# The last stage of a factorization kernel: x² times the summed W² as one level of Strassen's algorithm

## Chip, cores and metric

The kernel runs on one core of one Trainium2 chip. The metric is device time in microseconds (us) of one execution; the number for a kernel is the median of its runs.

## What is computed

x has 1024 rows and 512 features, the weight is 64 matrices W[e] of 512 x 512, all in float32. Cut to what matters:

```python
out_lin = x @ lin_w.T + lin_b
xv = jnp.einsum('bf,efm->bem', x, weight)
zp = jnp.einsum('bf,efm->bem', jnp.square(x), jnp.square(weight))
interaction = 0.5 * jnp.sum(jnp.square(xv) - zp, axis=1)
return out_lin + interaction
```

The sum over e of zp is one product: square(x) times the sum over e of square(W[e]). So the kernel computes 64 products x W[e], squares and adds them, and one more product, x² (sum of W²), at the end. The output is 1024 x 512: half the sum of squares, minus half of that last product, plus the linear layer.

## The kernel before

**Stages.** At the start come the linear layer (`lin`, L172) and the sums of blocks of x. Then a loop over 32 pairs of matrices (`q`, L404): a pair is one 512 x 1024 matrix, and x times it is done by two nested levels of Strassen's algorithm in the Winograd form, with 7 products instead of 8 at each level. The outer level has seven block products in the order "1265734" (L393), each of which consists of seven inner products named "1" to "7" (`block_product`, L288).

An inner product (`product`, L274) is two matmuls of 128 x 128 by 128 x 256 into the halves of one PSUM bank. A block product uses three banks, x, v and y, as running sums: "1" and "2" go to x, "5" and "3" to v, and y begins as a copy of x after "1" and then gains "6", "7" and "4". Between two products a bank is read out by ScalarE or VectorE (`out_of`, `join`), since the intermediate sums are blocks of the result. So a later product into a bank must wait until the earlier state has been read. PSUM has 2 buffers for tag x and 3 each for v and y.

GpSimd makes the sums of weight blocks (`outer_t` L226 for the outer level, `inner_t` L246 for the inner one), and it also issues the accumulating DMAs: the four finished blocks of a pair, z5, c11, c12 and c21, are squared in place by ScalarE (`squares`, L361) and then added to `acc[0]` (c11, c12) or `acc[1]` (z5, c21) by a DMA with an add. The squared weights (`w_squares`, L373) are added to `w2_sum` in the same manner. An accumulating DMA waits for the earlier one on the same destination.

**What sets the order.** Nothing is reordered by a scheduler: each piece of work is put in a list with a due time (`st.at(t, fn)`), the list is sorted by that time, and each engine receives its instructions in that order and works them off in order. One unit of due time is one inner product: a pair takes 49 units for its 49 products. The products of one block stand two units apart, and those of its neighbours lie between them. The last pair begins at 49 * 31, the list ends soon after 49 * 32. For the last block product of the last pair ("4", `t0` = 49 * 32 - 7) the list places its inner products at t0 + 0, 2, 4, 6, 8, 10 and 12, and the accumulations of z5, c12 and c21 five units after their squares.

**The last stage** follows the list (L453 to L478). x has been loaded again and squared (`load_xq`, `square_xq`, two instructions of 128 x 2048). For each of 8 blocks of 128 rows, four matmuls of 128 x 128 by 128 x 512 form the product (L462) in one of three banks of tag v. VectorE makes o = 0.5 acc + bias (L469) and then o - 0.5 ps (L477), and one DMA stores 128 rows of 2 KB (L478):

```python
nc.vector.scalar_tensor_tensor(o, ps, -0.5, o, ALU.mult, ALU.add)
nc.sync.dma_start(out_dst[:, n, :], o)
```

Tiles rotate through pools: `zpool` has 6 buffers, `spool` 3 of each tag, `w2pool` 2, `wpool` 4, `topool` 3.

Of the kernel before, what the change touches and what calls it, by code (L numbers as in the profile page):

```python
# [8 lines left out]
F32 = mybir.dt.float32  # L9
AF = mybir.ActivationFunctionType  # L10
ALU = mybir.AluOpType
# [17 lines left out]
def kernel(  # L29
# [30 lines left out]
    nc = tc.nc  # L60
    _, _, _, Q = x.shape
    E, F, M = weight.shape
    P = 128
    NK = F // P
    NB = 4 * Q // P
    HM = M // 2
    BK = 2 * HM

    const = ctx.enter_context(tc.tile_pool(name="const", bufs=1))
    wpool = ctx.enter_context(tc.tile_pool(name="wpool", bufs=4))  # L70
    topool = ctx.enter_context(tc.tile_pool(name="topool", bufs=3))
    tipool = ctx.enter_context(tc.tile_pool(name="tipool", bufs=3))
    w2pool = ctx.enter_context(tc.tile_pool(name="w2pool", bufs=2))
    spool = ctx.enter_context(tc.tile_pool(name="spool", bufs=3))
    zpool = ctx.enter_context(tc.tile_pool(name="zpool", bufs=6))
    psum = ctx.enter_context(
        tc.tile_pool(name="psum", bufs=3, space=bass.MemoryType.PSUM)
    )
# [4 lines left out]
    w2_sum = const.tile([P, NK, M], F32, tag="w2_sum", name="w2_sum")  # L83
    acc = [
        const.tile([P, 4, BK], F32, tag=f"acc{r}", name=f"acc{r}") for r in range(2)
    ]
# [4 lines left out]
    st = Stream()  # L91
# [7 lines left out]
    BLOCK = {"1": (0, 0), "2": (0, 1), "4": (1, 1)}  # L99
    a21 = {i: raw_sb[:, n, :] for n, i in enumerate("124")}  # L100
# [89 lines left out]
    def rows(n):  # L190

        r, s, j = n // 4, n // 2 % 2, n % 2
        return acc[r][:, 2 * s : 2 * s + 2, ts(j, HM)]
# [92 lines left out]
    Z = {}  # L286
# [74 lines left out]
    def squares(t, q, name, r):  # L361
        def sq():
            z = Z[q, name]
            for h in range(2):
                o = z[:, ts(h, 2)]
                nc.scalar.activation(o, o, AF.Square)  # L366

        st.at(t, sq)
        st.at(
            t + 5, lambda: nc.gpsimd.dma_start(acc[r], Z[q, name], accum_op=ALU.add)  # L370
        )

    def w_squares(t, q, v):  # L373
# [29 lines left out]
    NQ = E // 2  # L403
    for q in range(NQ):  # L404
        g0 = 49 * q
        st.at(-100 if q == 0 else g0 - 48.8, lambda q=q: load_w(q))
        for n, i in enumerate(ORDER):
            t0 = g0 + 7 * n
            lead = t0 - 7.5
            if i == "6":  # L410
                st.at(lead - 8, lambda q=q: outer_t(q, "5"))
                st.at(lead - 4, lambda q=q: outer_t(q, "6"))
            if i == "7":
                st.at(lead - 4, lambda q=q: outer_t(q, "7"))
            if i == "4":
                st.at(lead - 1, lambda q=q: outer_t(q, "4"))
            st.at(lead, lambda q=q, i=i: inner_t(q, i))
            block_product(t0, q, i, SUMS[i])
            if i == "2":
                squares(t0 + 14.6, q, "c11", 0)  # L420
            if i == "7":
                squares(t0 + 14.6, q, "z5", 1)
            if i == "3":
                squares(t0 + 14.6, q, "c12", 0)
            if i == "4":
                squares(t0 + 14.6, q, "c21", 1)
        for v in range(2):
            w_squares(g0 + 14.6 + 14 * v, q, v)
# [4 lines left out]
            st.at(t + 0.1 * n, fn)  # L433


    xq = []

    def load_xq():
        for r in range(2):
            xq.append(wpool.tile([P, 2, 4, Q], F32, tag="w", name=f"xq{r}"))  # L440
            nc.sync.dma_start(xq[r], x[:, ts(r, 2)])

    def square_xq(r):
        nc.scalar.activation(xq[r], xq[r], AF.Square)

    st.at(49 * NQ - 48.8, load_xq)
    for r in range(2):
        st.at(49 * NQ - 20 + 5 * r, lambda r=r: square_xq(r))

    with tc.manual_schedule():  # L450
        st.run()

    bias_sb = w2pool.tile([P, M], F32, tag="w2", name="bias_sb")  # L453
    nc.sync.dma_start(bias_sb, lin_b.partition_broadcast(P))
    out_dst = out.rearrange("(n p) m -> p n m", p=P)
    for n in range(NB):
        r, s, j = n // 4, n // 2 % 2, n % 2
        ps = psum.tile([P, M], F32, tag="v", name=f"ps_out{n}", bufs=3)
        o = spool.tile([P, M], F32, tag="s5", name=f"o{n}")
        for k in range(NK):  # L460
            kk, l = k // 2, k % 2
            nc.tensor.matmul(  # L462
                ps,
                xq[r][:, kk, (0, 1, 3, 2)[2 * s + l], ts(j, P)],
                w2_sum[:, k, :],
                start=(k == 0),
                stop=(k == NK - 1),
            )
        nc.vector.scalar_tensor_tensor(  # L469
            o.rearrange("p (u c) -> p u c", u=2),  # L470
            rows(n),
            0.5,
            bias_sb.rearrange("p (u c) -> p u c", u=2),
            ALU.mult,
            ALU.add,
        )
        nc.vector.scalar_tensor_tensor(o, ps, -0.5, o, ALU.mult, ALU.add)  # L477
        nc.sync.dma_start(out_dst[:, n, :], o)  # L478


# [28 lines left out]
```

## Time and profile before

| | |
|---|---|
| median of 3 runs | 1421.89 us (1421.57 to 1421.89) |
| the profiled execution | 1422.3 us, span 1420.5 us, granted TensorE clock 1.0 |
| last stage on TensorE (L462) | 1389.25 to 1416.73 us from the span's start, 64 records |
| last matmul of the pairs (L277) | starts within the group at 1388.15 us |
| GpSimd in the pairs' part, 50 to 1350 us | 1106.7 of 1300 us busy |
| GpSimd from 1395 us on | 0 busy |
| an accumulating DMA, issue to landing | 7.6 us (median of acc<-z_c) |

Times in views are us from the start of the span; a profile's row gives start, duration, engine, line, operation, the tiles (out<-in), the shape, how often, and in brackets how long the engine sat idle before and what ended that. PE is TensorE, DVE is VectorE, ACT is ScalarE, POOL is GpSimd, SP issues loads and stores. A float32 matmul leaves two MATMUL records. Matmuls overlap in the pipeline, so that the distance from start to start says more than the duration of one.

### The profile page before, as it was taken

The numbers are of one execution on the slowest core, as the hardware profiler recorded it, in microseconds if no ns is written. First come the engines' busy times: TensorE is split into PE (matmuls) and PEld (weight loads), VectorE is DVE, ScalarE is ACT, GpSimd is POOL, SyncE is SP. The second block draws the span as 40 slices with busy tenths as digits, with TensorE's granted clock in tenths as the row PEclk, the third lists the DMA queues.
The fourth block names the chain that finished last, engine by engine and source line by source line (L and its number), as shares of the span: only waits on it lengthen the run. The fifth ranks groups of instructions, "written<-read, shape, count | busy, mean of one in ns | idle before, by whom it ended". The sixth has DMA issues, their size and how long they took to land.

```text
span 1420.5 us, 17935 instructions
## 1 busy us (share of the span) xinstructions
PE 1415.3 (100%) x6408; PEld 1221.2 (86%) x6408; DVE 916.8 (65%) x1333; ACT 610.8 (43%) x811; POOL 1153.8 (81%) x1027
## 2 busy tenths in 40 slices
PE   9999999999999999999999999999999999999998
PEld 4888888888888888888888888888888888888884
DVE  7666666665666665666765666766666666566664
ACT  1444444444444445444345444344444444444451
POOL 4688888888888888988888888888888888888870
PEclk9999999999999999999999999999999999999999
DMA  4499898889998889888899988988988888988975
GB/s 177 107 194 215 198 202 200 187 191 216 200 201 202 184 197 214 198 200 198 194 193 203 207 200 197 201 186 194 215 200 200 200 187 189 217 200 200 202 161 148
DMA packets 39976, 276.15 MB, mean 194 GB/s; under 512 B 4432, under 2 KB 4816, under 8 KB 7248
## 3 DMA queue, kind: packets, MB, share of 16 engines
q0 software_dynamic: 27504, 200.29, 69.4%
q1 hardware_dynamic: 11808, 72.62, 17.2%
q10 hardware_dynamic: 576, 2.10, 0.4%
q8 instruction: 51, 0.84, 0.2%
q14 instruction: 37, 0.30, 0.1%
HBM read 72.61 MB, written 2.10 MB: 53 GB/s over the span
## 4 chain that ended last, share of the span: by engine, by line
PE 100%; DVE 0%; issue 0%
PE y L277 41%; PE x L277 27%; PE v L277 27%; PE ps_out L462 2%; PE lin L182 2%; PE y_spin L170 0%; DVE o L477 0%; DVE zero L167 0%
## 5 line engine op out<-in xcount | busy, mean ns | idle before, releaser
L277 PE MATMUL y<-ti,xs 128*128 128x256 f32 x2688 | 653.8, 379 | 0.0
L277 PEld LDWEIGHTS y<-ti,xs 128*128 128x128 f32 x2688 | 511.8, 190 | 68.8 <-issue 0.7
L342 ACT COPY y<-x 128x512 f32<-128x512 f32 x224 | 127.7, 570 | 622.8 <-PE x L277 622.8
L277 PE MATMUL x<-to,xs 128*128 128x256 f32 x1024 | 252.4, 379 | 0.0
L277 PE MATMUL v<-ti,xs 128*128 128x256 f32 x896 | 230.0, 379 | 0.0
L277 PEld LDWEIGHTS x<-to,xs 128*128 128x128 f32 x1024 | 195.0, 190 | 26.0
L251 POOL TENSOR_TENSOR ti<-to 128x512 f32<-128x512 f32 x128 | 180.7, 1412 | 44.2 <-PE y L277 40.7
L237 POOL TENSOR_TENSOR to<-w,to 128x1024 f32<-128x1024 f32 x64 | 158.9, 2483 | 45.7 <-PE v L277 45.7
L366 ACT ACTIVATE z_c<-z_c 128x1024 f32<-128x1024 f32 x192 | 192.7, 1053 | 3.1 <-DVE z_c L337 2.3
L277 PE MATMUL x<-w,xs 128*128 128x256 f32 x768 | 191.9, 379 | 0.0
L277 PEld LDWEIGHTS v<-ti,xs 128*128 128x128 f32 x896 | 170.6, 190 | 22.7
L337 DVE TENSOR_TENSOR z_z<-y,s 128x512 f32<-128x512 f32 x128 | 88.0, 687 | 130.4 <-PE y L277 130.4
L277 PEld LDWEIGHTS x<-w,xs 128*128 128x128 f32 x768 | 146.3, 190 | 19.9 <-issue 0.5
L251 POOL TENSOR_TENSOR ti<-w 128x512 f32<-128x512 f32 x96 | 130.9, 1364 | 30.6 <-PE y L277 20.2
L370 POOL DMA_DIRECT2D acc<-z_c x96 | 83.6, 871 | 63.7 <-ACT z_c L366 52.1
L277 PE MATMUL v<-to,xs 128*128 128x256 f32 x512 | 131.4, 379 | 0.0
L321 DVE TENSOR_TENSOR s<-y,z_z 128x512 f32<-128x512 f32 x160 | 110.3, 689 | 28.9 <-PE y L277 23.1
L382 ACT ACTIVATE w<-w 128x1024 f32<-128x1024 f32 x126 | 126.3, 1054 | 0.0
L337 DVE TENSOR_TENSOR z_c<-y,s 128x512 f32<-128x512 f32 x96 | 66.4, 692 | 87.9 <-PE y L277 87.9
L321 DVE TENSOR_TENSOR s<-v,z_z 128x512 f32<-128x512 f32 x160 | 110.1, 688 | 18.0 <-PE v L277 11.0
L337 DVE TENSOR_TENSOR z_z<-v,s 128x512 f32<-128x512 f32 x128 | 87.7, 685 | 38.6 <-PE v L277 38.6
L277 PEld LDWEIGHTS v<-to,xs 128*128 128x128 f32 x512 | 97.5, 190 | 13.0
(57 smaller groups left out, 1574.1 us busy)
## 6 DMA issues: line engine op xcount, KB each, us to landing
acc<-z_c POOLq DMA_DIRECT2D x96, 1024.0 KB, 7.6
w_sum<-w POOLq DMA_DIRECT2D x63, 1024.0 KB, 8.6
w<-weight SPq DMA_DIRECT2D x62, 1024.0 KB, 5.9
acc<-z_z POOLq DMA_DIRECT2D x32, 1024.0 KB, 7.7
xq<-x SPq DMA_DIRECT2D x2, 1024.0 KB, 5.6
out<-o SPq DMA_DIRECT2D x8, 256.0 KB, 2.0
xs<-x SPq DMA_DIRECT2D x3, 384.0 KB, 7.7
lw_sb<-lin_wT ACTq DMA_DIRECT2D x2, 512.0 KB, 6.6
```

Of the source, the lines that this page charges most:

```text
L182: nc.tensor.matmul(LIN[n], quarter(r, kk, (0, 1, 3, 2)[2 * s + l])[:, ts(j, P)], lw_sb[:, 2 * kk + l, :], start=(kk == 0 and l == 0), stop ...
L237: nc.gpsimd.tensor_sub(t, a, b)
L251: nc.gpsimd.tensor_sub(t[:, 0:2, :], b[:, :, HM:M], b.rearrange("p l m -> p (l m)")[:, 0:M].rearrange("p (u c) -> p u c", u=2),)
L277: nc.tensor.matmul(ps[:, ts(j, HM)], xsl(i, o)[:, ts(j, P)], rhs, start=(start and j == 0), stop=True, skip_group_check=True,)
L321: nc.vector.tensor_add(o, d[bank], Z[q, addend][:, blk])
L337: nc.vector.tensor_add(Z[q, name][:, blk], d[bank], d[s])
L342: st.at(t0 + 0.5, lambda: nc.scalar.copy(d["y"], d["x"]))
L366: nc.scalar.activation(o, o, AF.Square)
L370: t + 5, lambda: nc.gpsimd.dma_start(acc[r], Z[q, name], accum_op=ALU.add)
L382: nc.scalar.activation(w2[:, ts(h, 2)], W[q, v][:, ts(h, 2)], AF.Square)
L462: nc.tensor.matmul(ps, xq[r][:, kk, (0, 1, 3, 2)[2 * s + l], ts(j, P)], w2_sum[:, k, :], start=(k == 0), stop=(k == NK - 1),)
```

## The change

The last stage becomes one level of the same Winograd form, with x² cut into 2 x 2 blocks (rows r, features kk) and the sum of W² into 2 x 2 blocks (features kk, columns u). It is run twice, for the two halves s of the rows of a block. A product `last_product` is four matmuls of 128 x 128 by 128 x 256 (j over two groups of 128 rows, l over two of 128 features), so one half has 28 of them. Here P1 to P7 are its products, in the order 1, 5, 6, 2, 7, 3, 4; they use banks x, v, y as a block product does: P1 and P2 to x, P5 and P3 to v, y begins as ScalarE's copy of x after P1 and gains P6, P7 and P4.

- GpSimd computes the four sums of blocks of x² (`last_sx`, 128 x 1024 each) and the four of W² (`last_tw`, 128 x 512 each), at due times within the last pair. `last_sx` needs the squared x, `last_tw` the finished `w2_sum`.
- The list places the products of s=0 from g on (g = 49 * 32), the first ones between those of the last block "4", and those of s=1 from g + 10 on.
- For s=0, ScalarE reads the states v after P5, y after P6, x after P2 and y after P4 out, times -0.5 (`scaled`), and VectorE combines y after P7 and v after P3 with them (`minus_half`). Four `last_t` (0.5 acc + bias, for s=0) are added later by two `add_t` of 128 x 1024.
- For s=1, four `last_t` come first, and VectorE reads all six states out (`minus_half`), with t as addend where s=0 had none.
- In the VectorE list the four `last_t` of s=1 stand at g + 10.2, the six read-outs of s=1 at g + 12.5, 14.5, 16.5, 18.5, 20.5 and 22.5, and the `last_t` of s=0 and the `add_t` at g + 16.6 to 16.9.
- The bias has a buffer of its own and is loaded right after x. x² is squared in four instructions of 128 x 1024. For the last pair the accumulations stand two units after their squares, not five.
- A store is 128 x 2 rows of 1 KB; there are eight of them, as before.

```diff
--- before.py
+++ after.py
@@ -62,7 +62,6 @@
     E, F, M = weight.shape
     P = 128
     NK = F // P
-    NB = 4 * Q // P
     HM = M // 2
     BK = 2 * HM
 
@@ -367,7 +366,8 @@
 
         st.at(t, sq)
         st.at(
-            t + 5, lambda: nc.gpsimd.dma_start(acc[r], Z[q, name], accum_op=ALU.add)
+            t + (5 if q < NQ - 1 else 2),
+            lambda: nc.gpsimd.dma_start(acc[r], Z[q, name], accum_op=ALU.add),
         )
 
     def w_squares(t, q, v):
@@ -433,49 +433,166 @@
             st.at(t + 0.1 * n, fn)
 
 
-    xq = []
+    g = 49 * NQ
+    h = g - 49
+    XQ, SX, TW = [], {}, {}
+    bias = const.tile([P, M], F32, tag="bias", name="bias")
 
     def load_xq():
         for r in range(2):
-            xq.append(wpool.tile([P, 2, 4, Q], F32, tag="w", name=f"xq{r}"))
-            nc.sync.dma_start(xq[r], x[:, ts(r, 2)])
-
-    def square_xq(r):
-        nc.scalar.activation(xq[r], xq[r], AF.Square)
-
-    st.at(49 * NQ - 48.8, load_xq)
+            XQ.append(wpool.tile([P, 2, 4, Q], F32, tag="w", name=f"xq{r}"))
+            nc.sync.dma_start(XQ[r], x[:, ts(r, 2)])
+        nc.sync.dma_start(bias, lin_b.partition_broadcast(P))
+
+    def square_xq(r, kk):
+        nc.scalar.activation(XQ[r][:, kk], XQ[r][:, kk], AF.Square)
+
+    def last_x(i):
+        if i in BLOCK:
+            r, kk = BLOCK[i]
+            return XQ[r][:, kk]
+        return SX[i]
+
+    def last_sx(i):
+        if i in "57":
+            SX["tile" + i] = w2pool.tile([P, 2, 4, Q], F32, tag="w2", name=f"sx{i}")
+        SX[i] = SX["tile5" if i in "56" else "tile7"][:, "5673".index(i) % 2]
+        a21, a22 = XQ[1][:, 0], XQ[1][:, 1]
+        if i == "5":
+            nc.gpsimd.tensor_add(SX[i], a21, a22)
+        elif i == "6":
+            nc.gpsimd.tensor_sub(SX[i], SX["5"], last_x("1"))
+        elif i == "7":
+            nc.gpsimd.tensor_sub(SX[i], last_x("1"), a21)
+        else:
+            nc.gpsimd.tensor_sub(SX[i], last_x("2"), SX["6"])
+
+    def last_b(kk, u):
+        return w2_sum[:, ts(kk, 2), ts(u, HM)]
+
+    def last_tw(i):
+        if i in "57":
+            TW["tile" + i] = topool.tile([P, 2, 2, HM], F32, tag="to", name=f"tw{i}")
+        TW[i] = TW["tile5" if i in "56" else "tile7"][:, "5674".index(i) % 2]
+        a, b = {
+            "5": lambda: (last_b(0, 1), last_b(0, 0)),
+            "6": lambda: (last_b(1, 1), TW["5"]),
+            "7": lambda: (last_b(1, 1), last_b(0, 1)),
+            "4": lambda: (last_b(1, 0), TW["6"]),
+        }[i]()
+        nc.gpsimd.tensor_sub(TW[i], a, b)
+
+    def last_w(i):
+        if i in "123":
+            return last_b(*{"1": (0, 0), "2": (1, 0), "3": (1, 1)}[i])
+        return TW[i]
+
+    def last_product(ps, i, s, start):
+        for j in range(2):
+            for l in range(2):
+                nc.tensor.matmul(
+                    ps[:, ts(j, HM)],
+                    last_x(i)[:, (0, 1, 3, 2)[2 * s + l], ts(j, P)],
+                    last_w(i)[:, l, :],
+                    start=(start and j == 0 and l == 0),
+                    stop=True,
+                    skip_group_check=True,
+                )
+
+    out_dst = out.rearrange("(r s j p) (u c) -> r s p u j c", r=2, s=2, j=2, u=2)
+    L = {}
+
+    def last_banks(s):
+        for n in "xvy":
+            L[n, s] = psum.tile(
+                [P, BK], F32, tag=n, name=f"{n}_last{s}", bufs=2 if n == "x" else 3
+            )
+
+        L["o", s] = zpool.tile([P, 2, 2, BK], F32, tag="z", name=f"o_last{s}")
+        L["t", s] = zpool.tile([P, 2, 2, BK], F32, tag="z", name=f"t_last{s}")
+
+    def blk(n, s, b):
+        return L[n, s][:, b // 2, b % 2]
+
+    def last_p(i, bank, s, start):
+        return lambda: last_product(L[bank, s], i, s, start)
+
+    def last_t(s, r):
+        for u in range(2):
+            nc.vector.scalar_tensor_tensor(
+                L["t", s][:, r, u].rearrange("p (j c) -> p j c", j=2),
+                acc[r][:, 2 * s + u].rearrange("p (j c) -> p j c", j=2),
+                0.5,
+                bias[:, ts(u, HM)].unsqueeze(1).broadcast_to([P, 2, HM]),
+                ALU.mult,
+                ALU.add,
+            )
+
+    def scaled(bank, s, b):
+        return lambda: nc.scalar.activation(
+            blk("o", s, b), L[bank, s], AF.Copy, scale=-0.5
+        )
+
+    def minus_half(bank, s, b, addend):
+        def fn():
+            a = blk(addend, s, b)
+            nc.vector.scalar_tensor_tensor(
+                blk("o", s, b), L[bank, s], -0.5, a, ALU.mult, ALU.add
+            )
+
+        return fn
+
+    def store(s, b):
+        r, u = b // 2, b % 2
+        nc.sync.dma_start(
+            out_dst[r, s, :, u], blk("o", s, b).rearrange("p (j c) -> p j c", j=2)
+        )
+
+    def add_t(s, r):
+        nc.vector.tensor_add(L["o", s][:, r], L["o", s][:, r], L["t", s][:, r])
+        for u in range(2):
+            store(s, 2 * r + u)
+
+    st.at(g - 48.8, load_xq)
+    for n, (r, kk) in enumerate(((0, 0), (0, 1), (1, 0), (1, 1))):
+        st.at(h + 30.6 + 2.5 * (n // 2 * 2) + 0.1 * n, lambda r=r, kk=kk: square_xq(r, kk))
+    for i, t in zip("5673", (-8, -7.9, -3.8, -1)):
+        st.at(g + t, lambda i=i: last_sx(i))
+    for i, t in zip("5674", (-4, -3.9, -3.7, -0.9)):
+        st.at(g + t, lambda i=i: last_tw(i))
+    for s, ks in ((0, (0, 3.2, 5.2, 6, 7, 8, 9)), (1, (10, 12, 14, 16, 18, 20, 22))):
+        k1, k5, k6, k2, k7, k3, k4 = (g + k for k in ks)
+        st.at(k1 - 0.1, lambda s=s: last_banks(s))
+        st.at(k1, last_p("1", "x", s, True))
+        st.at(k1 + 0.5, lambda s=s: nc.scalar.copy(L["y", s], L["x", s]))
+        st.at(k5, last_p("5", "v", s, True))
+        st.at(k6, last_p("6", "y", s, False))
+        st.at(k2, last_p("2", "x", s, False))
+        st.at(k7, last_p("7", "y", s, False))
+        st.at(k3, last_p("3", "v", s, False))
+        st.at(k4, last_p("4", "y", s, False))
+
+        def put(bank, b):
+            return scaled(bank, s, b) if s == 0 else minus_half(bank, s, b, "t")
+
+        st.at(k5 + 0.5, put("v", 3))
+        st.at(k6 + 0.5, put("y", 1))
+        st.at(k2 + 0.5, put("x", 0))
+        st.at(k7 + 0.5, minus_half("y", s, 3, "o"))
+        st.at(k3 + 0.5, minus_half("v", s, 1, "o"))
+        st.at(k4 + 0.5, put("y", 2))
+        if s == 1:
+            for b, k in ((0, k2), (3, k7), (1, k3), (2, k4)):
+                st.at(k + 0.6, lambda b=b: store(1, b))
     for r in range(2):
-        st.at(49 * NQ - 20 + 5 * r, lambda r=r: square_xq(r))
+        st.at(g + 10.2 + 0.1 * r, lambda r=r: last_t(1, r))
+        st.at(g + 16.6 + 0.1 * r, lambda r=r: last_t(0, r))
+        st.at(g + 16.8 + 0.1 * r, lambda r=r: add_t(0, r))
 
     with tc.manual_schedule():
         st.run()
-
-    bias_sb = w2pool.tile([P, M], F32, tag="w2", name="bias_sb")
-    nc.sync.dma_start(bias_sb, lin_b.partition_broadcast(P))
-    out_dst = out.rearrange("(n p) m -> p n m", p=P)
-    for n in range(NB):
-        r, s, j = n // 4, n // 2 % 2, n % 2
-        ps = psum.tile([P, M], F32, tag="v", name=f"ps_out{n}", bufs=3)
-        o = spool.tile([P, M], F32, tag="s5", name=f"o{n}")
-        for k in range(NK):
-            kk, l = k // 2, k % 2
-            nc.tensor.matmul(
-                ps,
-                xq[r][:, kk, (0, 1, 3, 2)[2 * s + l], ts(j, P)],
-                w2_sum[:, k, :],
-                start=(k == 0),
-                stop=(k == NK - 1),
-            )
-        nc.vector.scalar_tensor_tensor(
-            o.rearrange("p (u c) -> p u c", u=2),
-            rows(n),
-            0.5,
-            bias_sb.rearrange("p (u c) -> p u c", u=2),
-            ALU.mult,
-            ALU.add,
-        )
-        nc.vector.scalar_tensor_tensor(o, ps, -0.5, o, ALU.mult, ALU.add)
-        nc.sync.dma_start(out_dst[:, n, :], o)
 
 
 def kernel(r_x, L0_rec_weight, L0_rec_lin_w, L0_rec_lin_b):
```

## Prediction

> **What bounds the kernel now.** I read the page first, then the chain of waits in order of time, then the timelines of the last 45 us engine by engine.
>
> ```profile
> span 1420.5 us, 17935 instructions
> PE 1415.3 (100%) x6408; PEld 1221.2 (86%) x6408; DVE 916.8 (65%) x1333; ACT 610.8 (43%) x811; POOL 1153.8 (81%) x1027
> PE 100%; DVE 0%; issue 0%
> ```
>
> TensorE never rests and the whole chain is TensorE's. So only the count of matmul columns, and what follows the last matmul, set the end. The change touches the last stage alone. In the chain it is one piece:
>
> ```profile
> 1389.25 27.48 PE ps_out L462 x64
> ```
>
> A float32 matmul appears as two records, so 32 matmuls give 64 records, 27.48 / 64 = 0.429 us apart. The products at L277 advance 8 records in 1.73 us (any "x8" piece of that chain), 0.216 each. VectorE's timeline of the tail:
>
> ```profile
> 1389.29 0.69 DVE L321 TENSOR_TENSOR z_c<-y,z_z 128x512 f32<-128x512 f32 x1 [0.42 <-PE y L277]
> 1396.79 1.29 DVE L469 SCALAR_TENSOR_TENSOR o<-acc,bias_sb 128x512 f32<-128x512 f32 x2 [6.81 <-DMA acc<-z_c]
> 1398.00 0.68 DVE L477 SCALAR_TENSOR_TENSOR o<-ps_out,o 128x512 f32<-128x512 f32 x1
> ...
> 1416.76 0.69 DVE L477 SCALAR_TENSOR_TENSOR o<-ps_out,o 128x512 f32<-128x512 f32 x1 [2.74 <-PE ps_out L462]
> ```
>
> VectorE stands 6.81 us for the accumulation of c12 into acc0, but TensorE has three banks for ps_out and hardly notices. At the end VectorE waits for TensorE. From the start of its last instruction to the end of the span are 3.74 us (0.69 plus 3.05 for the store). GpSimd and ScalarE:
>
> ```profile
> 1378.65 2.36 POOL L331 TENSOR_TENSOR z_z<-z_z,z_z 128x1024 f32<-128x1024 f32 x1 [0.50 <-DVE z_z L337]
> 1384.30 0.87 POOL L370 DMA_DIRECT2D acc<-z_z  x1 [3.28 <-issue]
> 1387.82 0.86 POOL L370 DMA_DIRECT2D acc<-z_c  x1 [2.65 <-ACT z_c L366]
> 1392.40 0.86 POOL L370 DMA_DIRECT2D acc<-z_c  x1 [3.72 <-DMA acc<-z_z]
> ```
>
> ```profile
> 1388.95 2.12 ACT L366 ACTIVATE z_c<-z_c 128x1024 f32<-128x1024 f32 x2 [1.43 <-DVE z_c L337]
> ```
>
> These three issues are z5, c12 and c21. By their times to landing in the DMA view (7.6, 8.9, 9.3) they land at 1391.9, 1396.7 and 1401.7: issued while another is moving, they come 4.8 to 5.0 us apart.
>
> **What the Trainium skill says.**
> - GPSIMD Engine Reference, section 3.1: a two-input elementwise operation costs about 2.6 cycles an element. 1024 elements take 2.36 us here, 2.36 x 1200 / 1024 = 2.8 of its 1.2 GHz cycles: agrees.
> - PSUM — Partial Sum Buffer, "Engine vs sequencer instructions": ScalarE, VectorE and GpSimd are strict FIFO. The tail of VectorE agrees: nothing passed the 6.81 us wait.
> - DMA: Bandwidth & Descriptors, "Rules for kernel authors": an accumulating DMA must wait for the earlier one on the same bytes. Agrees: c21 waited 3.72 us for z5.
> - TensorE: Matmul & The Clock Gate, "What's actually happening": after an idle window of about 3.4 us the array runs at half rate until it has been busy for such a window. The kernel's first eight records (L170) take 6.24 us, 0.78 each instead of 0.43, which agrees with a cold start; no idle of that length occurs later in this trace.
>
> **The change part by part.**
>
> *TensorE's work.* Away: 64 x 0.429 = 27.5 us. New: 2 halves x 7 products x 4 matmuls x 2 records = 112 x 0.216 = 24.2 us. Saved 3.3, and the first new products are interleaved with the last block's, which fills its small bubbles before 1389.09 (0.3 to 0.4). Were TensorE alone the limit, matmuls would end at about 1413.0 instead of 1416.7, and the end would come 3.7 us earlier.
>
> Laid out from 1385.38 (the last block's "2", undisturbed): P1 of s=0 at 1386.25, then "7", "3", P5 at 1389.7, "4" at 1391.4, P6 1392.3, P2 1394.0, P7 1395.75, P3 1397.5, P4 1399.2; for s=1 P1 1400.9, P5 1402.65, P6 1404.4, P2 1406.1, done at 1407.8.
>
> *GpSimd's sums.* Eight instructions after the last L331, which ends at 1381.0. Four of 128x1024 cost 2.36 each (rows L237, L331), four of 128x512 cost 1.3 with their gap (1.26 at L251; 1.56 right behind a DMA issue). In order: sx5 1383.3, sx6 1385.7, z5 issue (0.6), tw5 1387.9, tw6 1389.2, sx7 1391.5, tw7 1392.9, sx3 1395.2, tw4 1396.5. Their readers are P5 1389.7, P6 1392.3, P7 1395.75, P3 1397.5, P4 1399.2, so each is ready 1.8 us or more ahead: hidden under the products, and w2_sum has landed by 1383 (issue 1374.38 + 8.6). If GpSimd were half again slower, these margins would be gone and TensorE would stall about 4 us. What is not hidden: the accumulations queue behind the sums. z5 goes out at 1385.7 instead of 1384.3, c12 at 1396.5 instead of 1387.8.
>
> *ScalarE.* The c21 squares now stand behind three evacuations of s=0, the last of which needs P2's end (1395.9). They run from 1396.5 to 1398.5 instead of 1388.95 to 1391.1. So c21 is issued at 1398.8 instead of 1392.4. The squares of x (now four of 1.05 instead of two of 1.90) and the copies of y lie in idle time.
>
> *Landing of c21.* Pairs that overlapped: z5 to c12 took 12.4 us from the first issue to the second landing. From 1396.5 this gives 1408.9. Lower bound: as if alone, 1398.8 + 7.6 = 1406.4. Upper: another pair (issues 1349.83 and 1353.84, the second 9.3 to landing) took 13.3, giving 1409.8. I take 1408.9 because both move together.
>
> *The new wait.* In the compiled order, the four last_t of s=1 stand on VectorE behind s=0's two combinations and ahead of everything of s=1, and the last two read acc1, so they wait for c21. Behind them: v3, y1, x0 of s=1, four last_t of s=0, two add_t, y3, v1, y2. But P7 of s=1 accumulates in the bank that y1 reads, and P4 in the one that y3 reads, so TensorE waits too. After landing L, with 0.605 us from start to start for a 128x512 (L469, L477), 0.75 where an instruction needs the one just before, and for add_t 1.14 (two SBUF inputs took 0.42 for 256 and 0.95 for 768 elements early on with GpSimd quiet, about 1.03 ns an element): t(1,1) 0.07 and 0.67, v3 1.42, y1 2.0 to 2.7, x0 2.6, four last_t from 3.2, add_t 5.7 and 6.8, y3 7.95 to 8.65. P7 starts at L + 2.85 = 1411.8, about 4 us later than 1407.8. P4 starts at L + 8.8, its 8 records last 1.89, y2 runs from L + 10.75 to L + 11.45, the store needs 3.05: end = L + 14.5. Six of the eight stores now go out within 3 us ahead of the last one, in 1 KB rows instead of 2 KB: bounds 0 and 0.8, I take 0.2.
>
> *Sum.* 1408.9 + 14.7 = 1423.6 against 1420.5: 3.1 us later. The profiled execution took 1422.3 (its span and 1.8 around it), so 1425.4; it lay 0.4 above the median of 1421.89, so the median goes to **1425.0**, +0.22%.
>
> **The rivals.**
> - *TensorE goes cold.* P7 finds TensorE idle for 3.8 us. For: about the skill's window. Against: the window runs freely, so few gaps of 3.8 contain a whole one of 3.4. Price: P7 and P3 at half rate, 3.45 more; P4 could wait until L + 8.8 anyway, so 1.0 of it shows, or 2.7 if P4 is cold as well: 1426.0 to 1427.7.
> - *c21 lands early.* It ends at 1406.4, say because two overlapped DMAs move faster with no third behind them. Then the end is 1421.1: +0.6, 1422.5. Against: the pairs above. It is not slower in any measurable way for L up to 1408.6.
> - *The saving shows.* Mechanism: the accumulations land before VectorE needs them, and TensorE sets the end. It decides at L = 1402.7 (y3 then ends before P3 does at 1411.3): 1418.2. Break-even is L = 1405.8. For: c21 landed at 1401.7 before. Against: its squares wait for P2 on ScalarE, so it can't even be issued before 1398.5.
> - That the sums are late for their products: margins of 1.8 us or more stand against it, and it would add to the slower side.
>
> **How the numbers follow.** A measurement of this kernel can tell about 0.2%, 2.8 us, from no change. Forecast 0.60, its own range 1423.4 to 1426.2 (L and the stores at their bounds): slower 0.38, within 0.22. Cold 0.15, slower. Early landing 0.17, within. The saving 0.08: faster 0.06, within 0.02. Together faster 0.06, same 0.41, slower 0.53. The range reaches from just below the early landing (1422.2) to the cold case (1427.7) and leaves out the saving.
>
> **What would show it.** Right: 112 records 0.216 apart where TensorE runs; c12 and c21 issued near 1396.5 and 1398.8; a VectorE wait of some 4 us on "DMA acc<-z_c" ahead of last_t; TensorE idle about 4 us ahead of P7 and 2 ahead of P4, released by VectorE. Wrong: no idle on TensorE between 1386 and its end, c21 landing before 1406, or a wait of TensorE on POOL.

## The result and the profile after

The changed kernel takes 1426.34 us (median of 6 runs, 1424.76 to 1426.69) against 1421.89 (6 runs): ratio 1.0028, 95% interval 1.0015 to 1.0041. It is slower, by some 4.4 us. The profiled execution took 1426.34 with a span of 1424.6. First, three lines of its page:

```profile
span 1424.6 us, 18047 instructions
PE 1413.6 (99%) x6456; PEld 1231.4 (86%) x6456; DVE 918.7 (64%) x1335; ACT 614.1 (43%) x819; POOL 1168.0 (82%) x1035
PE 97%; DMA 1%; POOL 1%; issue 1%; DVE 0%; DVEq 0%; POOLq 0%
```

TensorE is busy for 1.7 us less than before, and yet the end is later: the chain that was TensorE's alone now has a DMA and GpSimd in it. Where it does is shown by the chain in order of time, near the end (start, duration, what):

```profile
1395.65 0.78 POOL acc L370
...
1398.08 11.66 DMA acc<-z_c
1409.74 0.02 issue
1409.76 1.30 DVE t_last L524 x2
```

The stage is ruled by the accumulation of c21, issued at 1398.08 and landed at 1409.74. TensorE's timeline, with P2, P7, P3 and P4 of s=1 in its last four lines:

```profile
1405.45 1.89 PE L495 MATMUL x_last<-w_sum,xq 128*128 128x256 f32 x8
1412.60 3.78 PE L495 MATMUL y_last<-tw,sx 128*128 128x256 f32 x8 [5.25 <-DVE o_last L541]
1416.17 2.56 PE L495 MATMUL v_last<-w_sum,sx 128*128 128x256 f32 x8
1418.57 1.90 PE L495 MATMUL y_last<-tw,xq 128*128 128x256 f32 x8
```

It idles 5.25 us before P7, until VectorE has read y. VectorE's timeline of the same stretch:

```profile
1402.65 1.29 DVE L524 SCALAR_TENSOR_TENSOR t_last<-acc,bias 128x512 f32<-128x512 f32 x2 [3.21 <-DMA acc<-z_c]
1409.76 1.29 DVE L524 SCALAR_TENSOR_TENSOR t_last<-acc,bias 128x512 f32<-128x512 f32 x2 [5.82 <-DMA acc<-z_c]
...
1411.86 0.68 DVE L541 SCALAR_TENSOR_TENSOR o_last<-y_last,t_last 128x512 f32<-128x512 f32 x1
1412.46 0.68 DVE L541 SCALAR_TENSOR_TENSOR o_last<-x_last,t_last 128x512 f32<-128x512 f32 x1
1413.06 2.49 DVE L524 SCALAR_TENSOR_TENSOR t_last<-acc,bias 128x512 f32<-128x512 f32 x4
1415.46 2.36 DVE L554 TENSOR_TENSOR o_last<-o_last,t_last 128x1024 f32<-128x1024 f32 x2
1417.73 0.69 DVE L541 SCALAR_TENSOR_TENSOR o_last<-y_last,o_last 128x512 f32<-128x512 f32 x1
```

What matters here is the order. The read-outs of v, y and x could have been done once P5, P6 and P2 had ended (1407.3 at the latest), but they stood behind last_t, which waited 5.82 us for c21. On GpSimd z5, c12 and c21 were issued at 1384.30, 1387.82 and 1392.40 before; now at:

```profile
1385.05 0.86 POOL L370 DMA_DIRECT2D acc<-z_z  x1
...
1394.38 1.27 POOL L485 TENSOR_TENSOR tw<-w_sum,tw 128x512 f32<-128x512 f32 x1
1395.59 0.84 POOL L370 DMA_DIRECT2D acc<-z_c  x1
1398.08 0.86 POOL L370 DMA_DIRECT2D acc<-z_c  x1 [1.65 <-ACT z_c L365]
```

**How to compare spans.** The pairs take the same time in all kernels, but their first product, which waits for the loads, starts at 34.13 to 35.46 us of the span (before 34.99, after 34.34), and the whole trace shifts with it. So each table row below also gives the time from the start of the last block's product "2" (1385.38 before, 1384.73 after) to the end of the span, which I call the tail.

| kernel | median us (runs) | ratio to before, 95% interval | span | product "2" | tail |
|---|---|---|---|---|---|
| before | 1421.89 (6) | | 1420.5 | 1385.38 | 35.1 |
| changed | 1426.34 (6) | 1.0028 (1.0015 to 1.0041) | 1424.6 | 1384.73 | 39.9 |
| e1_c12_first | 1422.59 (13) | 1.0005 (0.9997 to 1.0013) | 1421.4 | 1384.63 | 36.8 |
| e2_reads_first | 1423.94 (21) | 1.0013 (1.0007 to 1.0020) | 1422.7 | 1385.55 | 37.2 |
| e3_filler | 1428.01 (5) | 1.0036 (1.0023 to 1.0048) | 1426.3 | 1385.86 | 40.4 |
| e4_before_with_sums | 1430.44 (5) | 1.0058 (1.0044 to 1.0072) | 1428.3 | 1385.25 | 43.1 |
| e5_both_early | 1421.59 (13) | 0.9999 (0.9991 to 1.0007) | 1420.4 | 1385.62 | 34.8 |
| e6_early_and_order | 1419.72 (21) | 0.9984 (0.9978 to 0.9991) | 1418.3 | 1385.44 | 32.9 |
| e7_c21_late | 1427.36 (5) | 1.0035 (1.0022 to 1.0048) | 1424.4 | 1384.52 | 39.9 |
| e8_order_2 | 1418.98 (9) | 0.9978 (0.9968 to 0.9988) | 1417.3 | 1385.53 | 31.8 |

### The profile page after: what moved, and what is told of

Read it like the earlier page. It is cut to its first block, busy times and chain, and to the rows that moved or that the text cites. A ratio compares the mean times of both kernels' runs of the same rounds, so it can differ in the third digit from the quotient of the medians.

```text
span 1424.6 us, 18047 instructions
## 1 busy us (share of the span) xinstructions
PE 1413.6 (99%) x6456; PEld 1231.4 (86%) x6456; DVE 918.7 (64%) x1335; ACT 614.1 (43%) x819; POOL 1168.0 (82%) x1035
## 4 chain that ended last, share of the span: by engine, by line
PE 97%; DMA 1%; POOL 1%; issue 1%; DVE 0%; DVEq 0%; POOLq 0%
PE y L276 40%; PE x L276 27%; PE v L276 27%; PE lin L181 2%; DMA acc<-z_c 1%; DMA lw_sb<-lin_wT 0%; PE y_last L495 0%; POOL tw L485 0%; POOL sx L464 0%; POOL sx L466 0%; POOL sx L470 0%; PE v_last L495 0%; POOL acc L370 0%; DVE o_last L541 0%; POOL ti L250 0%
## 5 line engine op out<-in xcount | busy, mean ns | idle before, releaser
L250 POOL TENSOR_TENSOR ti<-to 128x512 f32<-128x512 f32 x128 | 180.8, 1413 | 43.2 <-PE y L276 39.9
```

What stands on the lines that cost most here:

```text
L250: nc.gpsimd.tensor_sub(t[:, 0:2, :], b[:, :, HM:M], b.rearrange("p l m -> p (l m)")[:, 0:M].rearrange("p (u c) -> p u c", u=2),)
```

## The experiments

The theory: the end follows the landing of c21, since VectorE works in order and last_t stands ahead of the read-outs that TensorE needs; c21 lands late because of where it stands on ScalarE and because c12, held up by the sums on GpSimd, still moves. The rivals: the Winograd chain of products and read-outs is too long in itself; the sums slow TensorE; the cold clock (TensorE at half its clock after an idle); the stores.

**e1_c12_first: c12 taken out from behind the sums.** On GpSimd its accumulation now stands between tw6 and sx7.

```diff
-                squares(t0 + 14.6, q, "c12", 0)
+                if q < NQ - 1:
+                    squares(t0 + 14.6, q, "c12", 0)
+                else:
+                    squares(t0 + 12.6, q, "c12", 0, 0.05)
-    for i, t in zip("5673", (-8, -7.9, -3.8, -1)):
+    for i, t in zip("5673", (-8, -7.9, -1.3, -1)):
-    for i, t in zip("5674", (-4, -3.9, -3.7, -0.9)):
+    for i, t in zip("5674", (-4, -3.9, -1.25, -0.9)):
```

(The last argument of `squares` is the distance of the accumulation from the squares in the last pair, 2 in the changed kernel.)

> The changed kernel with one move: c12 is squared ahead of ScalarE's copy of y, and its accumulation is issued on GpSimd ahead of sx7, tw7, sx3 and tw4, near 1388.5 us instead of 1395.6. c21 is untouched (issued near 1398.1). Theory (the end is the landing of c21 plus 14.7 to 14.9 us, since VectorE stands at last_t ahead of the read-outs that TensorE needs): c21 now moves alone, so it lands 7 to 7.6 us after its issue, 1405.1 to 1405.7 instead of 1409.7, TensorE's idle before P7 falls from 5.25 us to about 1, and the span goes from 1424.6 to about 1420.2, within 0.5 us of the kernel before. Rival (the serial chain of products and read-outs of the Winograd form sets the end): unchanged at 1424.6. Rival (the sums compete with TensorE's products): slower, as sx3 and tw4 now come 0.6 us later.

c12 went out at 1388.41, c21 at 1397.98 as before, and c21 landed 7.2 us later. TensorE's last lines:

```profile
1408.01 1.99 PE L498 MATMUL y_last<-tw,sx 128*128 128x256 f32 x8 [0.77 <-DVE o_last L544]
1409.84 1.89 PE L498 MATMUL v_last<-w_sum,sx 128*128 128x256 f32 x8
1413.88 3.58 PE L498 MATMUL y_last<-tw,xq 128*128 128x256 f32 x8 [2.15 <-DVE o_last L544]
```

The idle before P7 fell from 5.25 to 0.77 us and the tail by 3.1 us: both serial-chain and competing-sums rivals fall. Counted from product "2", c21 landed 4.5 us earlier than in the changed kernel. About 2.5 us of that come from c12 being out of the way; the rest is a late last part of the landing in the changed kernel, on which more below. The span missed the forecast by 1.2 us, and the last line says where: P4 took 3.58 us instead of 1.89, at half the clock.

**e2_reads_first: the accumulations as late as in the changed kernel, but nothing that TensorE needs behind them.** Both halves are read out alike (`put` is always `scaled`), and the rest is ordered so:

```diff
+    for k, fn, s, r in (
+        (10.2, last_t, 1, 0), (10.3, last_t, 0, 0), (10.4, add_t, 0, 0),
+        (20.6, last_t, 0, 1), (20.7, add_t, 0, 1), (20.8, last_t, 1, 1),
+        (20.9, add_t, 1, 0), (22.6, add_t, 1, 1),
+    ):
+        st.at(g + k, lambda fn=fn, s=s, r=r: fn(s, r))
```

> The changed kernel, but s=1 is read out as s=0 is: ScalarE reads v, y, x and y, VectorE's combinations need no accumulation, and what needs acc stands behind them (last_t for acc0 first, those for acc1 after the two combinations of s=1). The accumulations are issued as in the changed kernel. Theory: TensorE has no idle before P7 and P4 and ends at about 1412.4; c21 still lands at 1408 to 1409.7; behind it VectorE has four last_t and three add_t, about 6 to 7.5 us, and the store 3.4, so the span is about 1420 to 1421.5, 3 to 4.5 us below the changed kernel. Rival (GpSimd's sums themselves hold TensorE back, or the serial chain does): TensorE still idles and the span stays at 1424.6. If more than 1422.5 with no idle on TensorE, then the stores or add_t are the bound.

TensorE ran without an idle to its last product, which ended at 1413.34, 27.8 us after product "2" as forecast, though c12 and c21 were issued as late as in the changed kernel. c21 took 11.7 us to its landing here too (at 1410.6), so the accumulation was as late and TensorE no longer felt it: what had stopped TensorE was the wait on VectorE ahead of the read-outs. VectorE's last lines:

```profile
1411.65 0.69 DVE L541 SCALAR_TENSOR_TENSOR o_last<-v_last,o_last 128x512 f32<-128x512 f32 x1 [0.97 <-PE v_last L495]
1412.26 1.28 DVE L524 SCALAR_TENSOR_TENSOR t_last<-acc,bias 128x512 f32<-128x512 f32 x2
...
1415.92 2.35 DVE L554 TENSOR_TENSOR o_last<-o_last,t_last 128x1024 f32<-128x1024 f32 x2
```

The work behind c21 now comes after the products: VectorE ends at 1418.27 and the span 4.4 us later, at 1422.7, since six stores leave within 4 us. With the stage 0.85 us later than assumed, 1420.9 to 1422.4 had been forecast, with 3.4 us for the store; the 4.4 us account for the miss.

**e3_filler: TensorE kept busy in its wait.**

```diff
+    def filler():
+        ps = psum.tile([P, BK], F32, tag="v", name="v_filler", bufs=3)
+        for n in range(8):
+            nc.tensor.matmul(
+                ps[:, 0:HM], XQ[0][:, 0, 0, 0:P], w2_sum[:, 0, 0:HM], start=True, stop=True
+            )
+
+    st.at(g + 16.1, filler)
```

> The changed kernel with eight unused 128x256 matmuls (16 records, 3.45 us) on TensorE between P2 and P7 of s=1, while it waits[...]. Theory: P7 and P3 run at full rate (records 0.216 apart instead of 0.43), but P4 waits for y3, which stands behind four last_t and two add_t on VectorE, so the end moves by 0 to 0.3 us only. Rival (the cold clock is what makes the changed kernel slow): 1.5 to 3 us faster than the changed kernel.

```profile
1413.70 1.99 PE L495 MATMUL y_last<-tw,sx 128*128 128x256 f32 x8 [1.78 <-DVE o_last L541]
1415.53 1.89 PE L495 MATMUL v_last<-w_sum,sx 128*128 128x256 f32 x8
1419.57 2.76 PE L495 MATMUL y_last<-tw,xq 128*128 128x256 f32 x8 [2.15 <-DVE o_last L541]
```

P7 and P3 ran at the full clock, 1.99 and 1.89 instead of 3.78 and 2.56, and nothing was won: P4 then waited 2.15 us for VectorE. So the cold clock did not set the changed kernel's end. The tail is 0.5 us longer (40.4 against 39.9) where 0 to 0.3 had been forecast, as the clock fell in P4 instead, which took 2.76 us. The profiled execution was one of the slow ones here: the five lie between 1424.93 and 1428.12.

**e4_before_with_sums: GpSimd's sums alone, in the kernel before.** The eight sums are computed at the change's due times and read by nobody; the last stage is the plain one.

```diff
-            t + 5, lambda: nc.gpsimd.dma_start(acc[r], Z[q, name], accum_op=ALU.add)
+            t + (5 if q < NQ - 1 else 2),
+            lambda: nc.gpsimd.dma_start(acc[r], Z[q, name], accum_op=ALU.add),
...
+    for i, t in zip("5673", (-8, -7.9, -3.8, -1)):
+        st.at(g + t, lambda i=i: last_sx(i))
+    for i, t in zip("5674", (-4, -3.9, -3.7, -0.9)):
+        st.at(g + t, lambda i=i: last_tw(i))
```

> The kernel before with its plain last stage, to which only the eight sums on GpSimd are added at the places and due times of the change, with nobody reading them (the accumulations of the last pair two units after their squares, the bias in its own buffer, as in the change). Theory: the sums alone push c12's issue from 1387.8 to about 1396, it lands near 1403.5 instead of 1396.7, and TensorE runs out of its three banks at about 1399.5 and stands 5 to 6 us: span 1426 to 1429, 6 to 8 us slower than before, so the loss needs no Strassen. Rival (the loss comes from the bank reads of the Winograd form, the plain stage has slack for late accumulations): within 1 us of before.

```profile
1388.95 10.46 PE L506 MATMUL ps_out<-w_sum,xq 128*128 128x512 f32 x24
1405.09 19.46 PE L506 MATMUL ps_out<-w_sum,xq 128*128 128x512 f32 x40 [5.67 <-DVE o L521]
```

After three blocks (24 records) TensorE stood 5.67 us for a bank, because VectorE waited for c12, issued at 1396.12. The tail grew by 8.0 us, as forecast. Not all of it is the wait: the clock was granted at half from 1402.4 to 1409.2, and the 40 records behind the wait took 19.46 us, some 2 us more than at 0.429 us each. The sums ahead of the accumulations thus cost more in the plain stage than the whole change does; the tail of the changed kernel is 3.2 us shorter than this one.

**e5_both_early: c21 early as well.** As e1, and on ScalarE the squares of c21 stand ahead of the read-out of y, on GpSimd its accumulation ahead of tw4.

```diff
-                squares(t0 + 14.6, q, "c21", 1)
+                if q < NQ - 1:
+                    squares(t0 + 14.6, q, "c21", 1)
+                else:
+                    squares(t0 + 12.55, q, "c21", 1, 0.05)
-    for i, t in zip("5674", (-4, -3.9, -1.25, -0.9)):
+    for i, t in zip("5674", (-4, -3.9, -1.25, 5.65)):
```

> As e1_c12_first, and c21 too: its squares stand on ScalarE ahead of the read-out of y after P6, and its accumulation is issued ahead of tw4, near 1395.0 us instead of 1398.1 (times with the last block's product 2 at 1384.7, as in the changed kernel). Landing near 1402.0 to 1402.6. VectorE's order is as in the changed kernel. Theory (what counts is what stands ahead of a read-out on VectorE): the wait ahead of P7 is gone, but y3 still stands behind four last_t and two add_t, which begin only after x0, that is after P2 (1407.4), so y3 comes at 1412.8, TensorE idles about 2.7 us before P4, and the span is 1419.4 with a full clock in P4 or 1421 with half a clock there (as e1 showed): no more than 2 us below e1 though c21 lands 3 us earlier. Rival (the landing of c21 alone sets the end, at landing plus 14.7): 1416.9.

VectorE's wait for c21 ended at 1403.16, 7.3 us after its issue. The wait before P7 is gone:

```profile
1408.06 1.89 PE L501 MATMUL y_last<-tw,sx 128*128 128x256 f32 x8
1409.79 1.89 PE L501 MATMUL v_last<-w_sum,sx 128*128 128x256 f32 x8
1414.29 1.99 PE L501 MATMUL y_last<-tw,xq 128*128 128x256 f32 x8 [2.61 <-DVE o_last L547]
```

The span, 1420.4, is the forecast 1419.4 plus the 0.9 by which the stage starts later. The rival "landing plus 14.7" (1417.9) fails here: with an early landing another piece of the same order binds, y3 behind four last_t and two add_t.

**e6_early_and_order and e8_order_2: VectorE's order mended too.** e6 works off last_t and add_t ahead of the read-outs of s=1, acc0 first; e8 moves the last add_t behind v, y and x.

```diff
-        st.at(g + 10.2 + 0.1 * r, lambda r=r: last_t(1, r))
-        st.at(g + 16.6 + 0.1 * r, lambda r=r: last_t(0, r))
-        st.at(g + 16.8 + 0.1 * r, lambda r=r: add_t(0, r))
+        st.at(g + 10.2 + 0.3 * r, lambda r=r: last_t(1, r))
+        st.at(g + 10.3 + 0.3 * r, lambda r=r: last_t(0, r))
+        st.at(g + 10.4 + 0.3 * r, lambda r=r: add_t(0, r))  # e8: 10.4 + 6.2 * r
```

> As e5_both_early, and VectorE works off all last_t and add_t ahead of the read-outs of s=1, those for acc0 first, so that behind the landing of c21 only four last_t and one add_t (3.6 us) stand ahead of v3. Theory: v3, y1 and x0 come by 1407.9, TensorE does not idle by more than 0.5 us and ends at about 1412.5, y2 ends at 1413.2, the store adds 3.2 to 3.4: span 1416.4 to 1417, about 8 us below the changed kernel and 3 to 3.5 below the kernel before, which is the 3.7 us that the matmuls alone promised. Rival (the Winograd form's read-outs or the GpSimd sums bound the stage anyway): TensorE still idles, span 1419 or more.

> e6_early_and_order with the second add_t moved behind the read-outs of v, y and x of s=1, so that 2.4 instead of 3.6 us stand on VectorE between the landing of c21 and v3. Theory: y1 follows P6's end at once, TensorE's remaining idle before P7 (0.82 us in e6) goes, and the end comes 0.6 to 0.8 us earlier than e6: span about 1417.5 with the same start of the stage (1385.4), median 1418.9 to 1419.1. If the stores bunch again ahead of the last one, nothing is gained.

e6 idled 0.82 us before P7, where at most 0.5 had been forecast, and at 1418.3 it is 0.6 us above its forecast (1417.7 after the shift of 0.7), but 0.16% faster than the kernel before. In e8 TensorE has no idle left:

```profile
1407.98 1.89 PE L501 MATMUL y_last<-tw,sx 128*128 128x256 f32 x8
1409.70 1.89 PE L501 MATMUL v_last<-w_sum,sx 128*128 128x256 f32 x8
1411.43 1.89 PE L501 MATMUL y_last<-tw,xq 128*128 128x256 f32 x8
```

Its tail is 31.8 us, 3.3 below before; its median, 1418.98 (forecast: 1418.9 to 1419.1), is 0.22% or 2.8 us below that of the runs of before beside it (1421.82). By the tail that is nearly all of the 3.7 us that the count of matmuls had promised.

**e7_c21_late: c21 issued later.**

```diff
+    def spare():
+        t = wpool.tile([P, 2, 4, Q], F32, tag="w", name="spare")
+        for n in range(2):
+            nc.gpsimd.tensor_sub(t[:, n], XQ[0][:, 0], XQ[0][:, 1])
+
+    st.at(g + 5, spare)
```

> The changed kernel with two unused 128x1024 subtractions on GpSimd between the issues of c12 and c21, so that c21 is issued about 3.2 us later (near 1401.2 us instead of 1398.1, counted with the last block's product 2 at 1384.7). Theory (the landing sets the end, and a transfer that overlaps c12 lands late while one that does not takes 7.2 us, as in e1): c21 lands at 1408.4 to 1409.1, no later than in the changed kernel's profile (1409.7), and the span is landing plus 14.9, 1423.3 to 1424.0: 0 to 1.3 us below the changed kernel in spite of the later issue. Rival (the issue and its place on the GpSimd queue set the end): 3.2 us later, 1427.8.

c21 went out at 1400.62, 2.5 us later than in the changed kernel, and VectorE's wait ended at 1409.56: 25.0 us after product "2", as in the changed kernel. Span and tail are the same. So in these two profiles it is the landing that counts, not the issue. The forecast of a faster landing did not come true (8.9 us after the issue, not 7.2; fifteen of the sixteen parts of the landing did come within 7.2, at 1407.84). The median of the timed runs, 1427.36, is 1.0 us above the changed kernel's; the profiled execution was the fastest of its five. In this execution the rival's 3.2 us did not appear; more the run does not say.

## Why the prediction was right

- **The bound and the matmuls.** Right. The products of s=0 and the first four of s=1 run 0.216 us from record to record without a gap (P1 of s=1 at 1400.27, forecast 1400.9 less the 0.65 by which this trace starts earlier).
- **The sums on GpSimd.** Right: 2.36 and 1.27 us each; tw4 ended at 1395.65, P4 began at 1398.55. No product waited for them.
- **The issues.** c12 at 1395.59 (forecast, shifted, 1395.9) and c21 at 1398.08 (1398.15), with its squares on ScalarE behind the third read-out.
- **The landing of c21.** Mis-sized. From c12's issue to c21's landing I took 12.4 us, and 13.3 as the upper bound; it was 14.15, beyond the bound, so L came at 1409.74 instead of 1408.25 (shifted). This is where most of the missing microsecond lies: +1.5 for the landing, -0.65 for the start of the trace, 0.2 for the stores. The sum of the span was 1423.6, and 1424.6 was measured. What the term left out can be read from the trace, which records a landing in sixteen parts. Fifteen of c21's came by 1407.54, 11.95 us after c12's issue and so not later than forecast; the sixteenth came 2.2 us after them. Just there stands a 16 KB transfer of an instruction queue, from 1407.71 to 1408.66, and c21's last packet starts at 1408.64. The DMA view shows the transfer in the stretch 1406 to 1408.5 (first line) and that one packet from 1408.5 to 1412 (second line):

```profile
q8 instruction: 1, 0.02, 2.4%
DMA packets 1, 0.00 MB, mean 0 GB/s; under 512 B 1, under 2 KB 1, under 8 KB 1
```

In e2, e3 and e7 such a transfer also stands right before c21's last packets, and the last part comes 2.2, 2.2 and 1.7 us after the other fifteen; in the other six kernels none does, and the sixteen parts lie within 0.6 us. That the transfer is the cause is a reading of these ten traces: no run moves it by itself.

- **The new wait and the chain behind it.** Right: "end = L + 14.7" against 1424.6 - 1409.74 = 14.9. P4 at L + 8.8 was forecast and measured. TensorE's idle before P7 was 5.25 us, not 4, by the later landing; the second idle, 2 us before P4, did not appear, because P7 and P3 ran at half clock and filled it.
- **The cold rival.** The clock did go to half, to which I had given 0.15 and a price of 1.0 us or more, but it cost at most 0.1: y3 ended at 1418.42 and P4 began at 1418.57, against 0.06 us between the two in e3. The price was too high because the full clock was back at 1417.52, within P3. The argument against this rival was that few gaps of 3.8 us hold a whole window of 3.4. The gap was 5.25 us and all but filled one (1407.28 to 1410.69), and other runs show that less is enough (see the last section). The view by stretches shows the clock, in the column after POOL, then the DMA share and GB/s:

```profile
1412.00:1417.00 5.00, 4.40 (x10) 3.54 (x11) 5.00 (x8) 0.00 (x0) 0.00 (x0) 0.50 0.16 52
1418.00:1423.00 5.00, 2.47 (x12) 1.75 (x10) 1.80 (x3) 0.00 (x0) 0.00 (x0) 1.00 1.02 342
```

- **The stores.** 0.2 was taken. From VectorE's end to the end of the span are 3.4 us, 0.35 more than before. The second line fits this: the DMA engines are full from 1418 to 1423.
- **The total.** The median rose by 4.45 us where 3.1 was forecast. The profiled execution of before lay 0.4 above its median, that of the changed kernel on it; that is the other part of the difference. So 1426.34 lies just above 1423.4 to 1426.2, the range of the main case; the whole range holds it only because it reached up to the cold case, which cost next to nothing. That part is luck. And "slower" had been given 0.53, little more than even. The mechanism and the direction are not luck: with the late sixteenth part away, L would be about 1407.6 and the span about 1422.5 (an estimate, 1407.6 plus 14.9), still 2 us above before.

Two of the six runs of the changed kernel were 1.3 to 1.6 us faster than its median. A landing without the late sixteenth part would fit, but no trace of such a run was taken, so this stays open.

## What to carry to other kernels

When work is moved onto an engine that also issues DMAs, cost the issues behind it, not only the work: here eight sums that no product ever waited for made two accumulations late, and that cost 8 us in the plain stage, 5.7 of them a wait and some 2 the half clock behind it. Then look at who stands in order behind the wait for such a DMA; an instruction that frees a PSUM bank for the next product should not stand behind one that waits for a DMA. Saving matmuls pays only once issue, landing and read-out are put in the order in which the new stage needs them: the same products gave +4.4 us in one order and -2.8 in another.

## What the hardware showed that I had not expected

- TensorE's clock fell to half after shorter idles than the 3.4 us of the Trainium skill (TensorE: Matmul & The Clock Gate, "What's actually happening"). In e1 an idle of 2.15 us was followed by a P4 of 3.58 us, yet in e5 one of 2.61 us by a P4 of 1.99. The traces show what tells them apart. In all ten, the granted clock changes only at whole multiples of 3.413 us from the moment when it first becomes full: in the changed kernel it is half from 1410.69 to 1417.52, two such steps, in e1 from 1414.12 to 1417.53, one. What counts is the idle within one step. Below are two steps of e1 and one of e5; after the length comes PE's busy time and, behind POOL, the clock:

```profile
1410.71:1414.12 3.41, 1.26 (x6) 0.81 (x5) 3.41 (x5) 0.00 (x0) 0.00 (x0) 1.00 0.31 101
1414.12:1417.53 3.41, 3.33 (x8) 2.05 (x7) 0.34 (x2) 0.00 (x0) 0.00 (x0) 0.50 1.02 345
1409.94:1413.35 3.41, 1.74 (x9) 1.18 (x7) 3.41 (x5) 0.00 (x0) 0.00 (x0) 1.00 0.22 75
```

The idle of e1 lay within one step, 2.15 of its 3.41 us; that of e5 was split over two steps, with 1.67 us in the first and 0.94 in the second, and the clock stayed full. In the ten traces every step at full clock with 2.10 us or more of idle was followed by half clock, and none with 1.78 us (e3) or less. The steps begin at another time in each trace (the first at 4.4 to 7.5 us), so it is chance whether a step's end divides an idle.

- In the last 40 us of these traces an accumulating DMA of 1 MB landed 6.9 to 7.6 us after its issue when none was under way. Issued while another moved, it landed 4.9 to 5.5 us after that one, and some 2 us later still where an instruction transfer came before its last packet. Delaying the issue by 2.5 us in e7 moved fifteen parts of the landing by 0.5 us and the last not at all (counted from product "2").
